# Grouped queries laid 8 apart: moves of rotated halves in runs of 1 KB, score weights read with that stride

## The chip, the cores and the metric

The kernel runs on one core of a Trainium2 chip. Its time is the device time of one execution in microseconds (us). TensorE (PE in the profile) does the matrix products; each product consists of a load of its stationary operand (LDWEIGHTS, on the row PEld) and the stream of the moving operand through the array (MATMUL, on the row PE). VectorE (DVE), ScalarE (ACT) and GpSimd (POOL) do the rest, and SyncE (SP) issues most of the DMAs, one after the other in a queue of its own (SPq).

## The reference

Two layers over x of 16 sequences of 256 tokens and width 256, all in float32. Each layer computes `x + s * silu(f)` from the normalised x. In layer 0, s is a linear recurrence with 32 complex states and f a two-layer feed-forward network. In layer 1, s is causal attention with 16 heads and f a base product plus low-rank experts. What matters here is the attention of layer 1:

```python
q = (x @ Wq).reshape(B, S, N_HEADS, QK_DIM)
q_nope, q_rope = (q[..., :QK_NOPE], q[..., QK_NOPE:])
q = jnp.concatenate([q_nope, apply_rope(q_rope)], axis=-1)
...
scores = jnp.einsum('bqhd,bkhd->bhqk', q, k) * scale
mask = jnp.tril(jnp.ones((S, S), dtype=bool))
attn = jax.nn.softmax(scores, axis=-1)
out = jnp.einsum('bhqk,bkhd->bqhd', attn, v).reshape(B, S, N_HEADS * V_DIM)
```

The keys of all heads come from one latent of 64 numbers per token and one rotated part of 64, so that the kernel folds the head's key matrix into its query: a query is then 64 latent numbers and two rotated halves of 32, which makes 128 numbers, one per partition.

## The kernel before, in words

The 4096 tokens are cut into 8 chunks of 512 (two sequences each). Layer 0 runs first, for about 270 us; then layer 1 goes through the chunks. Each chunk has four **groups** of 4 heads, and each group has two **units**, one for each of the chunk's two sequences: 64 units in all. The program order of every engine is written out by hand: `InOrder` (lines 45 to 65) chains the instructions of an engine in the order in which they are written, and because it records each of them, nearly all of them carry line 53 in the profile. Instructions are therefore told apart by the tiles they write and read.

**Making the queries of a group** (lines 378 to 426). `query_mm` computes four products of 512 columns: t = 0 and 1 are the two rotated halves of the four heads (32 partitions for a head), t = 2 and 3 the latent parts of two heads each. `query_mul` (DVE) multiplies the rotary halves with cosines and sines; `query_rot` (POOL) adds and subtracts them into the tile `qrot`, of 2 x 512 numbers in each of 128 partitions. `query_lat` (ACT) scales the latent parts out of PSUM straight into the tile `qg`, partitions 0 to 63. The rotated halves lie in `qrot` with one head in 32 partitions, and must go to partitions 64 to 127 of `qg`, one head beside the other: `query_move` does that with eight DMAs on SP's queue, one for each half and head.

`qg` is laid out as 16 blocks of 32 queries, and within a block by head: `[P, CH // 32, G, 32]`. The 128 queries of one block and four heads lie next to each other, and a move writes runs of 32 numbers (128 bytes).

**Scores** (`score_pack`, lines 1354 to 1384). In a unit, block a of 32 queries needs the first 32 (a + 1) keys. The product has the 4 x 32 queries of the block as its stationary operand (a load of 128 columns) and the keys as its moving operand (32 to 256 columns). The eight blocks go in three packs, each into one PSUM bank: blocks 7 and 6; 5, 4 and 3; 2, 1 and 0. A float32 product is run as two passes, each with a load of its own, so that the profile has 1024 loads and 1024 matmuls for the 64 x 8 blocks. DVE then masks and takes the maxima, ACT the exponentials, POOL divides (`normalise`), DVE transposes squares of 32 x 32 (`turn`), and two DMAs by way of a DRAM buffer, `send` (lines 1411 to 1418) and `fetch` (line 1423), finish the transposition. `values` multiplies with the latents two units later, and `finish_mm` and `fast_mm` apply the output weights.

**Order** (the loop at lines 1603 to 1694). An even unit runs pack 0, `query_mm(n, 3)`, pack 1, the DMAs of `send` and then of `query_move`, `values` of two earlier units, pack 2. An odd unit runs pack 0, `query_mm(n, 0)`, pack 1, `query_mm(n, 1)`, pack 2, `query_mm(n, 2)`, and POOL does `query_rot` at its end. Smaller pieces (gates, routers, keys, the output product) stand between units. A group's queries are begun three units before its first pack 0. SP's queue holds, per unit, one fetch and four sends, and per group eight moves.

Of the kernel before, what the change touches and what calls it, by code (L numbers as in the profile page):

```python
# [11 lines left out]
F32 = mybir.dt.float32  # L12
I32 = mybir.dt.int32
AF = mybir.ActivationFunctionType
ALU = mybir.AluOpType
# [3 lines left out]
P = 128  # L19
B, S, D = 16, 256, 256  # L20
NTOK = B * S
CH = 512
# [19 lines left out]
def tile_two_layers(ctx: ExitStack, tc: tile.TileContext, d: dict, out: bass.AP):  # L42
# [158 lines left out]
    def bc(ap, n):  # L201

        return ap.unsqueeze(1).to_broadcast([ap.shape[0], n, ap.shape[1]])
# [11 lines left out]
    qr = ctx.enter_context(tc.tile_pool(name="qr1", bufs=1))  # L215
    qp = ctx.enter_context(tc.tile_pool(name="q1", bufs=2))
# [4 lines left out]
    gp = InOrder(nc.gpsimd)  # L221
    place = {}

    def m1(name, shape):
        return place["pool"].tile(shape, F32, tag=place["tag"], name=name)
# [142 lines left out]
    G = 4  # L368
    NG = NH // G
    NQ = S // 32  # L370
    SCALE = 1.0 / math.sqrt(NOPE + ROPE)
# [6 lines left out]
    def query_mm(n, t):  # L378
        q = groups[n]
        ch, g = divmod(n, NG)  # L380
        k = chunks[ch]
        if t == 0:
            q.qg = qp.tile([P, CH // 32, G, 32], F32, tag="qg", name=f"qg_{n}")
            q.rot = qr.tile([P, 2, CH], F32, tag="qrot", name=f"qrot_{n}")
            q.mul, q.ps = [None, None], [None] * 4
        q.ps[t] = ps = m1(f"pq_{n}_{t}", [P, CH])
        for c in range(2):
            if t < 2:
                w = wrope[:, c, g, t, :, :].rearrange("p h f -> p (h f)")
            else:  # L390
                h0 = g * G + 2 * (t - 2)
                w = wlat[:, c, h0 : h0 + 2, :]
            pe.matmul(ps, w, k.xnT[:, c, :], start=(c == 0), stop=(c == 1))

    def query_mul(n, t):
        q = groups[n]
        q.mul[t] = m = qm.tile([P, 2, CH], F32, tag="qmul", name=f"qmul_{n}_{t}")
        for r in range(2):
# [3 lines left out]
                bc(rot_q[:, r, :], 2), ALU.mult,  # L402
            )

    def query_lat(n, t):
        q = groups[n]
        for hh in range(2):
            ac.mul(
                q.qg[0:64, :, 2 * (t - 2) + hh, :],
                q.ps[t][64 * hh : 64 * hh + 64, :].rearrange("p (a q) -> p a q", q=32), SCALE,  # L410
            )

    def query_rot(n):
        q = groups[n]
        m0, m1_ = q.mul
        gp.tensor_tensor(q.rot[:, 0, :], m0[:, 0, :], m1_[:, 1, :], ALU.subtract)
        gp.tensor_tensor(q.rot[:, 1, :], m1_[:, 0, :], m0[:, 1, :], ALU.add)

    def query_move(n):
        q = groups[n]  # L420
        for r in range(2):
            for h in range(G):
                sp.dma_start(
                    q.qg[64 + 32 * r : 96 + 32 * r, :, h, :],
                    q.rot[32 * h : 32 * h + 32, r, :].rearrange("p (a q) -> p a q", q=32),
                )


    with ExitStack() as l0:
# [106 lines left out]
        def tiny(name, n=1):  # L536
            return w0.tile([P, n], F32, tag=name, name=name)
# [44 lines left out]
        f = tiny("f")  # L582
# [24 lines left out]
        for k in range(8):  # L607
            n = 1 << k
# [125 lines left out]
        def recur_out(ch, g, w, ve, ge):  # L734

            swapped(w, g)
            h = a2.tile([P, S], F32, tag="hs", name=f"hs_{ch}")
            ve.tensor_tensor(h, g, ct, ALU.mult)
            ge.tensor_tensor(h, h, w, ALU.subtract)
            return h  # L740
# [476 lines left out]
        o = out1  # L1217
        for ch in range(FIRST, NCH - 1):
            xn, xnT, norm2, o = middle(ch, xn, xnT, norm2, fill, o)
# [5 lines left out]
        t = 2 * ch - 1  # L1225
# [27 lines left out]
        h = recur_out(ch, g, w, v0, g0)  # L1253
        zf = mix(ch, 0, hT, v=v0, a=a0)
        router_chunk(0)
        key_chunk(0)
        outs(ch, h, dx, v0)
        query_mm(0, 0)
        query_mul(0, 0)
        query_mm(0, 1)  # L1260
        query_mul(0, 1)
        finish0(ch, 0, dx, zf, g0)
        query_rot(0)
        query_move(0)
        for jp in range(2):
            finish0(ch - 1, jp, z6.dx, z6.z[jp], v0)
        zf = mix(ch, 1, hT, v=v0, a=a0)
        ve.tensor_scalar(bb_bc, bb_bc, 0.5, None, ALU.mult)
        query_mm(0, 2)
        query_lat(0, 2)  # L1270
        query_mm(0, 3)
        query_lat(0, 3)
        norm_end(1)
        query_mm(1, 0)
        query_mul(1, 0)
        query_mm(1, 1)
        query_mul(1, 1)
        finish0(ch, 1, dx, zf, g0)
        query_rot(1)
        query_mm(1, 2)  # L1280
        query_lat(1, 2)


# [70 lines left out]
    def score_pack(u, pi):  # L1354
        k, b, pack = chunks[u.ch], u.b, PACK[pi]
        if pi == 0:
            u.nm = sm1.tile([P, NQ], F32, tag="nm", name=f"nm_{u.n}", bufs=3)
            u.sr = sm1.tile([P, NQ], F32, tag="sr", name=f"sr_{u.n}", bufs=3)
        qg = groups[u.i // 2].qg
        sc = ps_sc.tile([P, CH], F32, tag="sc", name=f"sc_{u.n}_{pi}")  # L1360
        for a, o in pack:
            pe.matmul(
                sc[:, o : o + 32 * (a + 1)], qg[:, b * NQ + a, :, :].rearrange("p h q -> p (h q)"),
                k.kT[:, b * S : b * S + 32 * (a + 1)], start=True, stop=True,
            )
        ends = [o + 32 * (a + 1) for a, o in pack]
        step = ends[1] - ends[0]
        n = len(pack)
        assert ends == [ends[0] + step * z for z in range(n)]
        if ends[0] - 32 + step * n <= CH:  # L1370
            diag = sc[:, ends[0] - 32 : ends[0] - 32 + step * n].rearrange("p (n s) -> p n s", n=n)[:, :, 0:32]
        else:
            diag = sc[:, ends[0] - step : ends[-1]].rearrange("p (n s) -> p n s", n=n)[:, :, step - 32 : step]
        ve.tensor_tensor(diag, diag, bc(kmask, n), ALU.add)
        for a, o in pack:
            ve.tensor_reduce(
                u.nm[:, a : a + 1], sc[:, o : o + 32 * (a + 1)], AX.X, ALU.max, negate=True
            )
        for a, o in pack:
            w = 32 * (a + 1)  # L1380
            ac.activation(
                u.pr[:, OFF[a] : OFF[a] + w], sc[:, o : o + w], AF.Exp,
                bias=u.nm[:, a : a + 1], accum_out=u.sr[:, a : a + 1],
            )
# [218 lines left out]
    for i in range(LAST):  # L1603
        ch, r = divmod(i, PER)
# [3 lines left out]
        n = (i + 3) // 2 if odd else (i + 2) // 2  # L1608
        n = n if n < len(groups) else None
# [4 lines left out]
        if 2 <= i:  # L1614
            fetch(units[i - 2])
        score_pack(u, 0)
        if w:
            normalise(w, (2,))
# [30 lines left out]
        if i == 5:  # L1649
            values(units[1])  # L1650
        score_pack(u, 1)

        if odd and n is not None:
            query_mm(n, 1)
            query_mul(n, 0)
        if i == 2:
            query_move(n)
# [6 lines left out]
        if not odd:  # L1664
            if n is not None and i != 2:
                query_move(n)
            if i >= 4:
                values(units[i - 4])
            if i > 4:
                values(units[i - 3])  # L1670
        score_pack(u, 2)
        normalise(u, (0, 1))

        if odd and n is not None:
            query_mm(n, 2)
            query_mul(n, 1)
            query_rot(n)
            query_lat(n, 2)
# [111 lines left out]
```

## Time and profile before

| | |
|---|---|
| time, median of 3 runs | 921.83 us (920.75 to 923.23) |
| span of the profiled execution | 919.9 us |
| PE busy | 905.2 us, 98% of the span |
| PEld busy | 695.4 us, 76% |
| DVE, ACT, POOL busy | 72%, 51%, 62% |
| idle time of PE within the span | 14.7 us |
| DMA packets | 196412, of which 142112 are under 512 bytes |

The profile is of one execution, and its span is the time from its first to its last instruction. The page gives no other time of that execution; the median of the runs shown is 1.9 us above the span. PE's clock is granted in full from the first slices on (9 of 9 in tenths, 0.98 to 1.00 in every stretch after 60 us). The DMA engines are nearly idle between 60 and 270 us, and about 73% busy from 340 to 880 us. A busy share of PE is not a share of its peak: matmuls overlap, so the time that one of them adds is read from the distance between the starts of two, not from its own duration.

### The profile page before, as it was taken

The numbers are of one execution on the slowest core, as the hardware profiler recorded it, in microseconds if no ns is written. First come the engines' busy times: TensorE is split into PE (matmuls) and PEld (weight loads), VectorE is DVE, ScalarE is ACT, GpSimd is POOL, SyncE is SP. The second block draws the span as 40 slices with busy tenths as digits, with TensorE's granted clock in tenths as the row PEclk, the third lists the DMA queues.
The fourth block names the chain that finished last, engine by engine and source line by source line (L and its number), as shares of the span: only waits on it lengthen the run. The fifth ranks groups of instructions, "written<-read, shape, count | busy, mean of one in ns | idle before, by whom it ended". The sixth has DMA issues, their size and how long they took to land.

```text
span 919.9 us, 17382 instructions
## 1 busy us (share of the span) xinstructions
PE 905.2 (98%) x5426; PEld 695.4 (76%) x5426; DVE 666.4 (72%) x2018; ACT 465.8 (51%) x1529; POOL 570.6 (62%) x885
## 2 busy tenths in 40 slices
PE   8999999999999899999999999999999999999998
PEld 7768898987767567777777777777777777777776
DVE  6876687664688779668967866896786689677562
ACT  3335555654336545645644564564466456446541
POOL 1228697777355537686586767648676764866541
PEclk9999999999999999999999999999999999999999
DMA  9730000000025777777776777777677777767771
GB/s 280 232 115 1 1 2 1 1 2 1 1 32 106 201 203 184 203 186 186 178 210 160 208 194 192 189 178 207 159 209 206 181 190 178 205 160 211 206 224 42
DMA packets 196412, 134.00 MB, mean 146 GB/s; under 512 B 142112, under 2 KB 186976, under 8 KB 196320
## 3 DMA queue, kind: packets, MB, share of 16 engines
q1 hardware_dynamic: 194192, 128.68, 53.3%
q0 software_dynamic: 1152, 3.67, 1.2%
q8 instruction: 44, 0.72, 0.3%
q10 hardware_dynamic: 976, 0.53, 0.2%
q14 instruction: 48, 0.39, 0.1%
HBM read 63.11 MB, written 52.95 MB: 126 GB/s over the span
## 4 chain that ended last, share of the span: by engine, by line
PE 90%; DVE 3%; DMA 2%; SPq 2%; POOL 1%; issue 1%; ACT 0%; POOLq 0%; DVEq 0%; ACTq 0%
PE pq L53 22%; PE sc L53 14%; PE po L53 10%; PE av L53 9%; PE r L53 7%; PE f L53 7%; PE ph L53 5%; PE pf L53 5%; PE pg L53 4%; PE pm L53 2%; SPq L53 2%; PE pkv L53 1%; PE tp L53 1%; DMA qg<-qrot 1%; PE py L53 1%; PE pb L53 1%
## 5 line engine op out<-in xcount | busy, mean ns | idle before, releaser
L53 ACT ACTIVATE pr<-sc,nm 128x256 f32<-128x256 f32 (+7 forms) x512 | 189.7, 381 | 240.3 <-DVE sr L53 152.2
L53 POOL TENSOR_SCALAR pr<-pr,sr 128x256 f32<-128x256 f32 (+7 forms) x512 | 192.1, 394 | 190.0 <-DVE sr L53 184.1
L53 PEld LDWEIGHTS sc<-kT,qg 128*128 128x128 f32 x1024 | 157.6, 191 | 62.3 <-issue 40.3
L53 PE MATMUL sc<-kT,qg 128*128 128x256 f32 (+7 forms) x1024 | 176.1, 306 | 5.7 <-DMA qg<-qrot 4.4
L53 DVE TENSOR_REDUCE nm<-sc 128x1 f32<-128x256 f32 (+7 forms) x512 | 127.5, 301 | 6.6
L53 DVE STREAM_TRANSPOSE turned<-pr 128x512 f32<-128x512 f32 x186 | 123.2, 687 | 9.6 <-POOL pr L53 8.7
L53 PE MATMUL pq<-xnT,wlat 128*128 128x512 f32 x256 | 124.1, 608 | 0.0
L53 PE MATMUL pq<-xnT,wrope 128*128 128x512 f32 x256 | 120.2, 593 | 0.0
L53 ACT ACTIVATION_READ_ACCUMULATOR pr<-sc,nm 128x1 f32 x512 | 104.3, 204 | 0.0
L53 DVE TENSOR_TENSOR sc<-sc,kmask 128x96 f32<-128x96 f32 (+1 forms) x192 | 45.5, 237 | 64.9 <-PE sc L53 63.9
L53 PE MATMUL av<-pT,row 128*64 128x256 f32 (+1 forms) x1024 | 90.9, 329 | 0.5 <-DMA pT<-far 0.5
L53 POOL TENSOR_TENSOR qrot<-qmul,qmul 128x512 f32<-128x512 f32 x64 | 83.0, 1317 | 8.0 <-POOL pr L53 2.9
L53 PEld LDWEIGHTS av<-pT,row 128*64 128x64 f32 x1024 | 64.1, 137 | 24.3 <-issue 1.6
L53 DVE TENSOR_TENSOR qmul<-pq,rot_q 128x512 f32<-128x512 f32 x128 | 80.7, 672 | 0.1
L53 ACT ACTIVATE qg<-pq 64x512 f32<-64x512 f32 x128 | 75.4, 589 | 5.4 <-PE pq L53 4.7
L53 PEld LDWEIGHTS pq<-xnT,wlat 128*128 128x128 f32 x256 | 46.0, 192 | 32.0 <-issue 32.0
L53 PEld LDWEIGHTS pq<-xnT,wrope 128*128 128x128 f32 x256 | 45.7, 191 | 32.4 <-issue 32.1
L53 PEld LDWEIGHTS po<-wout,attT 128*128 128x128 f32 x416 | 58.4, 191 | 9.5 <-issue 4.9
L53 PE MATMUL po<-wout,attT 128*128 128x128 f32 (+1 forms) x416 | 64.5, 308 | 0.0
L53 POOL TENSOR_TENSOR rs<-ve,mhalf 128x4 f32<-128x4 f32 (+1 forms) x17 | 16.8, 986 | 51.3 <-DVE ve L53 37.0
L53 PE MATMUL ph<-xnT,p1T 128*128 128x256 f32 (+1 forms) x128 | 44.3, 503 | 0.8 <-DVE xnT L53 0.8
L53 POOL TENSOR_TENSOR attT<-attT,attT 128x512 f32<-128x512 f32 x36 | 45.0, 1270 | 0.0
(226 smaller groups left out, 1505.0 us busy)
## 6 DMA issues: line engine op xcount, KB each, us to landing
far<-turned SPq DMA_DIRECT2D x248, 192.0 KB, 4.3
pT<-far SPq DMA_DIRECT2D x62, 768.0 KB, 5.0
qg<-qrot SPq DMA_DIRECT2D x256, 64.0 KB, 2.3
x<-in_x_dram SPq DMA_DIRECT2D x7, 512.0 KB, 9.3
out_dram<-x POOLq DMA_DIRECT2D x12, 256.0 KB, 4.9
wqn_wo<-in_wq_nopeT_dram SPq DMA_DIRECT2D x4, 512.0 KB, 4.9
wqn_wo<-in_Wo_dram SPq DMA_DIRECT2D x4, 512.0 KB, 6.1
p2T<-in_proj2T_dram SPq DMA_DIRECT2D x2, 512.0 KB, 7.2
```

The source lines that it names most:

```text
L53: r = getattr(self.engine, name)(*args, **kw)
```

## The change

`qg` becomes `[P, 2, G, S]`: for each sequence and head a run of 256 queries in each partition, with query 32 a + q at place 8 q + a. The 32 queries of block a are thus 8 numbers (32 bytes) apart. `qrot` takes the same order, so that a move copies runs of 256 numbers (1 KB) on both sides. The 128 stationary columns of a score product (four heads of 32 queries) are then read with a step of 8 numbers; the step goes on evenly from one head to the next, since a head is 256 = 32 x 8 numbers long. ACT (`query_lat`) and POOL (`query_rot`) read as before, block after block, and write with a step of 8 numbers. Number, kind and order of the instructions of all engines stay as they are.

```diff
         if t == 0:
-            q.qg = qp.tile([P, CH // 32, G, 32], F32, tag="qg", name=f"qg_{n}")
-            q.rot = qr.tile([P, 2, CH], F32, tag="qrot", name=f"qrot_{n}")
+            q.qg = qp.tile([P, 2, G, S], F32, tag="qg", name=f"qg_{n}")
+            q.rot = qr.tile([P, 2, 2, S], F32, tag="qrot", name=f"qrot_{n}")
...
+    def strided(ap):
+
+        return ap.rearrange("p b (q a) -> p b a q", a=NQ)
+
+    def blocks(ap):
+
+        return ap.rearrange("p (b a q) -> p b a q", b=2, q=32)
+
     def query_lat(n, t):
         q = groups[n]
         for hh in range(2):
             ac.mul(
-                q.qg[0:64, :, 2 * (t - 2) + hh, :],
-                q.ps[t][64 * hh : 64 * hh + 64, :].rearrange("p (a q) -> p a q", q=32), SCALE,
+                strided(q.qg[0:64, :, 2 * (t - 2) + hh, :]),
+                blocks(q.ps[t][64 * hh : 64 * hh + 64, :]), SCALE,
             )
 
     def query_rot(n):
         q = groups[n]
         m0, m1_ = q.mul
-        gp.tensor_tensor(q.rot[:, 0, :], m0[:, 0, :], m1_[:, 1, :], ALU.subtract)
-        gp.tensor_tensor(q.rot[:, 1, :], m1_[:, 0, :], m0[:, 1, :], ALU.add)
+        r0, r1 = (strided(q.rot[:, r]) for r in range(2))
+        gp.tensor_tensor(r0, blocks(m0[:, 0, :]), blocks(m1_[:, 1, :]), ALU.subtract)
+        gp.tensor_tensor(r1, blocks(m1_[:, 0, :]), blocks(m0[:, 1, :]), ALU.add)
 
     def query_move(n):
...
                 sp.dma_start(
-                    q.qg[64 + 32 * r : 96 + 32 * r, :, h, :],
-                    q.rot[32 * h : 32 * h + 32, r, :].rearrange("p (a q) -> p a q", q=32),
+                    q.qg[64 + 32 * r : 96 + 32 * r, :, h, :], q.rot[32 * h : 32 * h + 32, r]
                 )
...
             pe.matmul(
-                sc[:, o : o + 32 * (a + 1)], qg[:, b * NQ + a, :, :].rearrange("p h q -> p (h q)"),
+                sc[:, o : o + 32 * (a + 1)],
+                qg[:, b].rearrange("p h (q a) -> p a (h q)", a=NQ)[:, a],
                 k.kT[:, b * S : b * S + 32 * (a + 1)], start=True, stop=True,
             )
```

## The prediction

> **What bounds the kernel now.** I read the page's busy times first, then TensorE's waits, then the chain of work through two units.
>
> ```profile
> PE 905.2 (98%) x5426; PEld 695.4 (76%) x5426; DVE 666.4 (72%) x2018; ACT 465.8 (51%) x1529; POOL 570.6 (62%) x885
> ```
>
> TensorE (PE) is busy all but 14.7 us of the 919.9 us span, and no other engine comes near. Its waits:
>
> ```profile
> PE sc L53 <- DMA qg<-qrot: 4.4, 2, 3.5
> ...
> PE sc L53 <- ACT pr L53: 1.3, 1, 1.3
> ...
> PE av L53 <- DMA pT<-far: 0.5, 1, 0.5
> ```
>
> The moves that the change speeds up make TensorE wait twice, for 4.4 us in all, both times before 400 us. Everything DMA costs TensorE is 4.9 us. So the change can gain half a per cent at most, and what matters is whether it makes TensorE's own work longer. The chain (start, us, what) shows how that work is spaced in an odd unit:
>
> ```profile
> 350.53 0.81 PE sc L53 x4
> 351.34 1.72 PE pq L53 x4
> 353.06 0.82 PE sc L53 x6
> 353.88 1.72 PE pq L53 x4
> 355.60 0.59 PE sc L53 x6
> ```
>
> The four pq matmuls stream 512 columns each and take 1.72 us: 0.84 ns per column. By that, pack 0 (256, 256, 224, 224 columns) needs 0.81 us and pack 1 (192, 160, 128, each twice) also 0.81; the chain has 0.81 and 0.82. Pack 2 (96, 64, 32, each twice) would need 0.32 but takes 0.59: it waits for its weight loads.
>
> ```profile
> 355.44 0.64 PEld L53 LDWEIGHTS sc<-kT,qg 128*128 128x128 f32 x5 [0.24 <-issue]
> 355.99 0.30 PEld L53 LDWEIGHTS pq<-xnT,wlat 128*128 128x128 f32 x2
> ```
>
> Five loads start within 0.55 us, 110 ns apart. A load runs beside the matmul ahead of it, so a step from one matmul to the next lasts as long as the longer of that matmul's stream and the next load.
>
> **Part 1, the strided weights.** 1024 loads of 128 columns now read words 32 bytes apart. Contiguous loads cost, by form:
>
> ```profile
> L53 PEld LDWEIGHTS sc<-kT,qg 128*128 128x128 f32 x1024 | 157.6, 191 | 62.3 <-issue 40.3 <-ACT pr L53 8.5 <-ACT qg L53 4.3
> L53 PEld LDWEIGHTS av<-pT,row 128*64 128x64 f32 x1024 | 64.1, 137 | 24.3 <-issue 1.6 <-PE av L53 0.7
> ```
>
> 64 more columns take 191 - 137 = 54 ns: 0.84 ns per column, 108 for the load. No row of this trace has an operand of the array with a step, so the price needs bounds.
> - Below: 0.84 ns per column as now. Nothing is gained, since the columns are as many.
> - Above: one further fetch per column, as slow as the slowest word in any row. GpSimd's two-input operations need (1267 - 726) / 256 = 2.11 ns per element for two words (rows below), 1.06 per word. 0.84 + 1.06 = 1.90 ns, 243 ns a load.
> - I take a second fetch at the array's own pace, 2 x 0.84 = 1.69 ns, 216 ns a load. With the step no two columns of a load lie side by side, and the nearest row with two fetches per element is GpSimd's 2.11.
>
> [...]
>
> With loads of 216 ns, by the step rule, at 0.84 ns per column:
> - Pack 0: streams 215, 215, 188, 188; the following loads 216, 216, 216 and a contiguous 108. Steps 216 x 3 + 188 = 836 ns, 30 more than 806.
> - Pack 1: five steps of 216 and a last of 108 make 1188, 382 more than 806.
> - Pack 2: five of 216 and one of 108 make 1188; before, six of 108 were 648. 540 more.
> - The first load of a pack. Ahead of pack 1 always, and of pack 2 in odd units, stands a pq stream of 430 ns: hidden. Ahead of pack 2 in even units stand the `values` matmuls (2.75 us for 32): 108 more, 54 on average. Ahead of pack 0 stand 128-column matmuls (108 ns streams) in 6 of 8 units: 81 on average.
>
> Sum 1087 ns per unit; 64 units: **+69.6 us**, all on TensorE's path. At the ends: nothing, and, at 243 ns, 111 + 517 + 675 + 108 + 68 = 1479 ns, +94.7 us.
>
> **Part 2, the moves.** Each of 256 issues becomes cheaper on SP's queue. I compare the moves with the four loads of `rot_q`, which have the shape of the new moves (32 partitions with runs of 1 KB):
>
> ```profile
> L53 SPq DMA_DIRECT2D qg<-qrot x256: 585/628/2102, 261.6 to 878.7; - x128
> ...
> L165 SPq DMA_DIRECT2D rot_q<-in_rope_q_dram x4: 414/420/582, 30.2 to 31.7; - x4
> ```
>
> About 0.21 us less each, 1.5 us over the seven issues between a move's first and last. Packets fall from 512 per move to 64, 114688 fewer of 196412. The waits of 3.5 and 0.9 us become 2.0 and 0: a gain of 2.4. Landing takes 2.3 us now and 1.9 for `rot_q`; with less traffic for all others the ends are -2.4 and all DMA waits, -4.9. With an unchanged TensorE I take the middle, **-3.6**. If part 1 slows TensorE by a microsecond per unit, everything that feeds it is earlier by that, and both waits on the moves go: **-4.4**.
>
> [...]
>
> **Part 3, strided writes of ACT and POOL.** Rows now:
>
> ```profile
> L53 ACT ACTIVATE qg<-pq 64x512 f32<-64x512 f32 x128 | 75.4, 589 | 5.4 <-PE pq L53 4.7
> ```
>
> ```profile
> L53 POOL TENSOR_TENSOR qrot<-qmul,qmul 128x512 f32<-128x512 f32 x64 | 83.0, 1317 | 8.0 <-POOL pr L53 2.9 <-DVE qmul L53 2.8 <-DMA qg<-qrot 2.2
> ...
> L53 POOL TENSOR_SCALAR pr<-pr,sr 128x256 f32<-128x256 f32 x64 | 30.6, 478 | 133.8 <-DVE sr L53 128.0 <-DMA qg<-qrot 4.1 <-DMA pT<-far 0.5
> ...
> L53 POOL TENSOR_TENSOR c<-c,g 128x256 f32<-128x256 f32 x12 | 8.7, 725 | 0.0
> ```
>
> Nothing below today's time is possible, since elements and passes stay. Above, one more 0.84 ns for each of 512 elements is +0.43 us: 128 x 0.43 = 55 us on ACT, 64 x 0.43 = 28 us on POOL. I take the upper end and cost it at nothing: on ACT the exponentials queued behind wait 240.3 us in all for DVE, on POOL the divisions 190.0 us, and a group's queries are begun three units before use. Per group ACT would work 1.7 us more in about 20 us. If the cover is gone, up to 55 us come to the end; maxima and PSUM banks for scores would be late next.
>
> **The sum.** On the profiled execution: 919.9 + 69.6 - 4.4 = 985.1. The median of the runs is 1.9 above the span: **987.0 us**.
>
> **Rivals.**
> 1. *Strided loads cost nothing* (the other side). The moves are then all that changes: 921.8 - 3.6 = 918.2, between 916.9 and 919.4. For it: a load takes one word per column at 0.84 ns, contiguous or not, and no row shows that neighbours help. Against it: every row of the trace reads neighbours. Per nanosecond of longer load a unit loses 5 (pack 2), 1 (the end of pack 1) and 1.25 (first loads); 3.6 us over 64 units are 56 ns, so it decides at a load of 116 ns, 0.90 ns per column.
> 2. *Half a fetch more*, midway between none and one: 162 ns. Pack 0 stays, pack 1 +112, pack 2 +270, first loads +67: 449 ns per unit, 28.7 us, 946 us. For it: part of a fetch may lie under the one before. [...]
> 3. *The cover of part 3 is gone*: up to 55 us with free loads, 973. Against it: ACT and POOL idle for hundreds of microseconds.
> 4. *The moves gain nothing* because TensorE hardly waits for them and their landing is a fixed cost; with free loads that is 921.8.
>
> **Numbers.** Forecast 0.40, rival 1 0.35, rival 2 0.14, rival 3 and loads beyond 243 ns 0.08, rival 4 0.03. Range: from rival 1's lower end, 916, to the bound of 243 ns, 921.8 + 94.7 - 4.4 = 1012. Alone, the forecast's case is 975 to 1012. A difference under 0.3%, 2.8 us, cannot be told from no change. Rival 1 straddles that at 919.1: 0.26 faster, 0.09 same. With rival 4: faster 0.26, same 0.12, slower 0.62.
>
> **What would show it.** The mean of the score loads: 191 ns now, about 299 if right, 191 in rival 1. The chain's packs: 0.84, 1.19 and about 1.13 us against 0.81, 0.82, 0.59; only packs 1 and 2 may grow, and matmul rows of pq stay at 1.72 per four. Move issues near 420 ns; packets near 82000; TensorE's waits for `qg` gone. `qg` near 1.02 us on ACT at most. I am wrong if the score loads keep 110 ns of spacing, or if TensorE shows new idle time behind ACT or DVE.

## The result, and the profile after

The changed kernel takes 1000.71 us (median of 4 runs, 1000.18 to 1001.77) against 922.53 us (median of 4 runs beside it): 1.0848 times the time before, with a 95% interval of 1.0833 to 1.0864. It is 78 us slower. The forecast was 987.0 us, in a range of 916 to 1012.

The page's busy times and TensorE's waits in the changed kernel:

```profile
PE 988.9 (99%) x5426; PEld 797.3 (80%) x5426; DVE 664.7 (67%) x2018; ACT 535.2 (54%) x1529; POOL 573.0 (57%) x885
```

```profile
PE tp L53 <- DVE xn L53: 1.9, 1, 1.9
PE warm L53 <- POOL ident masks.py:199: 1.5, 1, 1.5
PE pmT L53 <- ACT qg L53: 1.4, 1, 1.4
PE ph L53 <- DVE xnT L53: 0.8, 1, 0.8
```

The span grew from 919.9 to 998.4 us, by 78.5. TensorE's busy time grew by 83.7 us and its idle time fell by 5.2. No wait for a move is left, and no new wait behind DVE, ACT or POOL has come; the one that grew is that of `pmT` for ACT's part of a query, from 0.5 to 1.4 us. TensorE did not get its work later, the work itself got longer. The chain shows which work (start, us, what; an odd unit again):

```profile
357.30 0.93 PE sc L53 x4
358.23 1.72 PE pq L53 x4
359.94 1.30 PE sc L53 x6
361.24 1.72 PE pq L53 x4
362.96 1.22 PE sc L53 x6
```

The pq products are where they were, at 1.72 us for four. The three packs of scores went from 0.81, 0.82 and 0.59 us to 0.93, 1.30 and 1.22. Pack 2, with the shortest streams, was the shortest and now takes nearly as long as pack 1: both have six loads, and the streams no longer count. The weight loads say so themselves (timelines of the load row and of the matmul row, and the groups by form):

```profile
362.37 1.69 PEld L53 LDWEIGHTS sc<-kT,qg 128*128 128x128 f32 x6 [0.24 <-issue]
363.97 0.32 PEld L53 LDWEIGHTS pq<-xnT,wlat 128*128 128x128 f32 x2
```

```profile
362.80 1.38 PE L53 MATMUL sc<-kT,qg 128*128 128x96 f32 x6
```

```profile
L53 PEld LDWEIGHTS sc<-kT,qg 128*128 128x128 f32 x1024 | 265.2, 330 | 39.2 <-issue 21.3 <-ACT pr L53 3.7 <-DVE eq L53 1.7
L53 PEld LDWEIGHTS av<-pT,row 128*64 128x64 f32 x1024 | 64.0, 137 | 23.7 <-issue 1.6
```

The first of the six loads lies beside a stream of 512 columns; the chain starts the pack at 362.96, and the timeline has its first matmul at 362.80. The other five start between there and 363.97, where the next load follows: 234 ns each, where it was 110. The mean load went from 191 to 330 ns. The loads of `av`, which are contiguous, stayed at 137.

The issues of the moves (min, median and max of one in ns), the page's line of DMA packets, and its groups of the two engines that now write with a step:

```profile
L53 SPq DMA_DIRECT2D qg<-qrot x256: 585/595/1835, 261.1 to 951.9; - x128
```

```profile
DMA packets 81724, 134.00 MB, mean 134 GB/s; under 512 B 11040, under 2 KB 72288, under 8 KB 81632
```

```profile
L53 ACT ACTIVATE qg<-pq 64x512 f32<-64x512 f32 x128 | 141.4, 1105 | 2.3 <-PE pq L53 1.5
...
L53 POOL TENSOR_TENSOR qrot<-qmul,qmul 128x512 f32<-128x512 f32 x64 | 81.7, 1300 | 2.8 <-DVE qmul L53 2.8
```

The packets fell by 114688 as counted, yet an issue takes 595 ns in the median where it took 628, not 420. ACT's writes nearly doubled (589 to 1105 ns); POOL's hardly changed (1317 to 1300).

### The profile page after: what moved, and what is told of

Same layout as the page of the kernel before. It is cut to its first block, busy times and chain, and to the rows that moved or that the text cites. A ratio compares the mean times of both kernels' runs of the same rounds, so it can differ in the third digit from the quotient of the medians.

```text
span 998.4 us, 17382 instructions
## 1 busy us (share of the span) xinstructions
PE 988.9 (99%) x5426; PEld 797.3 (80%) x5426; DVE 664.7 (67%) x2018; ACT 535.2 (54%) x1529; POOL 573.0 (57%) x885
## 3 DMA queue, kind: packets, MB, share of 16 engines
q1 hardware_dynamic: 79504, 128.68, 44.6%
## 4 chain that ended last, share of the span: by engine, by line
PE 98%; DVE 1%; DMA 0%; ACT 0%; POOL 0%; issue 0%; SPq 0%; POOLq 0%
PE sc L53 24%; PE pq L53 22%; PE po L53 10%; PE av L53 9%; PE r L53 6%; PE f L53 6%; PE ph L53 4%; PE pg L53 4%; PE pf L53 4%; PE pm L53 2%; PE pkv L53 2%; PE tp L53 1%; PE py L53 1%; PE pb L53 1%; PE psq L53 1%; PE pso L53 0%
## 5 line engine op out<-in xcount | busy, mean ns | idle before, releaser
L53 POOL TENSOR_SCALAR pr<-pr,sr 128x256 f32<-128x256 f32 (+7 forms) x512 | 195.5, 401 | 264.1 <-DVE sr L53 262.6
L53 PEld LDWEIGHTS sc<-kT,qg 128*128 128x128 f32 x1024 | 265.2, 330 | 39.2 <-issue 21.3
L53 PE MATMUL sc<-kT,qg 128*128 128x256 f32 (+7 forms) x1024 | 262.8, 391 | 0.0
L53 ACT ACTIVATE qg<-pq 64x512 f32<-64x512 f32 x128 | 141.4, 1105 | 2.3 <-PE pq L53 1.5
L53 DVE TENSOR_TENSOR sc<-sc,kmask 128x96 f32<-128x96 f32 (+1 forms) x192 | 47.5, 248 | 139.7 <-PE sc L53 138.1
L53 ACT ACTIVATION_READ_ACCUMULATOR pr<-sc,nm 128x1 f32 x512 | 102.1, 199 | 0.0
```

The lines of the kernel that those rows point to most:

```text
L53: r = getattr(self.engine, name)(*args, **kw)
```

## The experiments

The theory, called S: a load whose columns do not lie side by side takes longer for each column, and that alone makes the difference. Its refinement, L, an assumption of the author's until the steps were run (e4 to e6): what counts is how many columns fall into one piece of 16 bytes (a line, in the expectations). The first rivals put the longer loads down to something else that the change brought (W), or the loss to ACT's longer writes (A).

### One part alone: the loads (e1), and all but the loads (e2)

e1 is the kernel before, with

```diff
-                sc[:, o : o + 32 * (a + 1)], qg[:, b * NQ + a, :, :].rearrange("p h q -> p (h q)"),
+                sc[:, o : o + 32 * (a + 1)], qg[:, b * NQ : (b + 1) * NQ].rearrange("p a h q -> p (a h q)").rearrange("p (c z) -> p z c", z=8)[:, a],
```

> The kernel before with one change: a score load reads its 128 columns with a step of 8 numbers (32 bytes). It thereby takes columns of eight blocks at once, so that the scores are those of other queries; their number and the work are the same. Moves, ScalarE and GpSimd as before. Theory S (the step of the read alone makes the load longer): mean of the score loads 330 ns as after, packs 0, 1 and 2 near 1.0, 1.3 and 1.2 us, time 998 to 1006 us. Rival W (the loads are longer because of who writes the tile now: ScalarE's writes with a step and moves of 1 KB that collide with the loads): loads 191 ns, time 920 to 925 us.

e2 is the changed kernel, with

```diff
-                qg[:, b].rearrange("p h (q a) -> p a (h q)", a=NQ)[:, a],
+                qg[:, b].rearrange("p h s -> p (h s)")[:, P * a : P * (a + 1)],
```

> The changed kernel with one thing undone: a score load reads 128 adjacent columns. It thereby takes other queries than those of its block; their number and the work are the same. The moves of 1 KB and the strided writes of ScalarE and GpSimd stay. Theory S: loads 191 ns, time 916 to 922 us, although ScalarE's writes into qg stay at 1.1 us. Rival W: loads 330 ns, time about 1000 us. Rival A (ScalarE's longer writes delay the exponentials): loads 191 ns, TensorE has new idle time, time 930 to 975 us.

Measured: e1 1000.49 us, 1.0847 [1.0824, 1.0871]; e2 919.85 us, 0.9967 [0.9955, 0.9980]. The loads by form, of e1 and then of e2:

```profile
L53 PEld LDWEIGHTS sc<-kT,qg 128*128 128x128 f32 x1024 | 265.2, 330 | 39.2 <-issue 21.1 <-ACT pr L53 3.8 <-DVE eq L53 1.7
```

```profile
L53 PEld LDWEIGHTS sc<-kT,qg 128*128 128x128 f32 x1024 | 157.7, 191 | 60.4 <-issue 40.2 <-ACT pr L53 12.0 <-DVE eq L53 1.7
```

The step of the read alone gives the whole ratio of the change, 1.0847 beside 1.0848, and everything else in the change gives a small gain. W has fallen: in e1 the tile is written as before and the loads take 330 ns; in e2 it is written as after and they take 191. e1 and the changed kernel also show that once TensorE is slow, the moves are worth nothing that can be seen: their times lie 0.2 us apart, with runs of 128 bytes and of 1 KB, and e1 has no wait for a move either.

A has fallen as well: 919.85 us is below the 930 that it asks for at least. In e2 ACT's writes take as long as in the changed kernel, 1102 ns in the median, and TensorE's waits are few:

```profile
PE sc L53 <- ACT pr L53: 2.9, 2, 2.7
...
PE pmT L53 <- ACT qg L53: 1.5, 1, 1.5
...
PE sc L53 <- DMA qg<-qrot: 1.0, 1, 1.0
```

A write takes 593 ns in the median before, so that the 128 of them keep ACT 65 us longer in e2, and TensorE's waits behind ACT grow by no more than 2.6 us (2.9 and 1.5 us here, 1.3 and 0.5 before, the last in this row of the kernel before):

```profile
PE pmT L53 <- ACT qg L53: 0.5, 1, 0.5
```

### The moves alone (e3)

```diff
-            q.qg = qp.tile([P, CH // 32, G, 32], F32, tag="qg", name=f"qg_{n}")
+            q.qg = qp.tile([P, 2, G, S], F32, tag="qg", name=f"qg_{n}")
...
-                q.ps[t][64 * hh : 64 * hh + 64, :].rearrange("p (a q) -> p a q", q=32), SCALE,
+                q.ps[t][64 * hh : 64 * hh + 64, :].rearrange("p (b s) -> p b s", b=2), SCALE,
...
-                    q.rot[32 * h : 32 * h + 32, r, :].rearrange("p (a q) -> p a q", q=32),
+                    q.rot[32 * h : 32 * h + 32, r, :].rearrange("p (b s) -> p b s", b=2),
...
-                sc[:, o : o + 32 * (a + 1)], qg[:, b * NQ + a, :, :].rearrange("p h q -> p (h q)"),
+                sc[:, o : o + 32 * (a + 1)], qg[:, b].rearrange("p h s -> p (h s)")[:, P * a : P * (a + 1)],
```

> The kernel before with the moves alone changed: qg and qrot in the plain order of the tokens, runs of 1 KB in the moves, contiguous writes of ScalarE and GpSimd, and score loads of 128 adjacent columns (of other queries than those of the block; the work is the same). What the moves are worth without their price: 916.9 to 919.4 us by the prediction's first rival, TensorE's 4.4 us of waits for the moves gone or below 2. Rival M (the moves gain nothing): 921 to 923 us, the waits as before.

Measured: 918.05 us, 0.9942 [0.9924, 0.9961]. This is what the change could have brought: 5.6 us, within its interval 3.6 to 7.0. TensorE's waits:

```profile
PE sc L53 <- DMA qg<-qrot: 2.3, 1, 2.3
```

Half of the 4.4 us of waits for moves went, where below 2 us had been expected to stay. The issues got only 33 ns cheaper and landing went from 2.3 to 2.0 us, so that moves still come late once. The 5.6 us are a difference of medians; the two profiled executions differ by 2.7 us (spans of 919.9 and 917.2), and what else the medians contain was not traced. The difference between e2 and e3 (what the strided writes of ACT and POOL cost) lies within the intervals of the two, which overlap, and is not shown.

### How the price depends on the step (e4, e5, e6)

Each is e1 with another step. In place of e1's new line stands, for 2, 3 and 4:

```diff
+                sc[:, o : o + 32 * (a + 1)], qg[:, b * NQ : (b + 1) * NQ].rearrange("p a h q -> p (a h q)").rearrange("p (w c z) -> p w z c", z=2, c=P)[:, a % 4, a % 2],
+                sc[:, o : o + 32 * (a + 1)], qg[:, b * NQ : (b + 1) * NQ].rearrange("p a h q -> p (a h q)")[:, 0:3 * P].rearrange("p (c z) -> p z c", z=3)[:, a % 3],
+                sc[:, o : o + 32 * (a + 1)], qg[:, b * NQ : (b + 1) * NQ].rearrange("p a h q -> p (a h q)").rearrange("p (w c z) -> p w z c", z=4, c=P)[:, a % 2, a % 4],
```

> As e1 with a step of 2 numbers (8 bytes; scores of other queries, the same work). [...] Rival G (the price grows with the step): loads 205 to 240 ns, time 930 to 955 us. Rival N (any step other than 1 costs the same): loads 330 ns, about 1003 us.

> As e1 with a step of 3 numbers (12 bytes; scores of other queries, the same work). [...] Rival T (a step under 16 bytes is free, as step 2 nearly was): loads 197 ns, 922 to 926 us.

> As e1 with a step of 4 numbers (16 bytes; scores of other queries, the same work). Theory L: every column opens a line, as with step 8: loads 330 ns, time 998 to 1003 us. Rival G (the price grows with the distance): loads 220 to 280 ns, 930 to 970 us.

The rows of the loads, of e4, e5 and e6 in turn:

```profile
L53 PEld LDWEIGHTS sc<-kT,qg 128*128 128x128 f32 x1024 | 162.7, 197 | 60.0 <-issue 39.6 <-ACT pr L53 8.8 <-ACT qg L53 4.2
```

```profile
L53 PEld LDWEIGHTS sc<-kT,qg 128*128 128x128 f32 x1024 | 206.4, 258 | 48.5 <-issue 34.9 <-ACT pr L53 10.2 <-DVE eq L53 1.7
```

```profile
L53 PEld LDWEIGHTS sc<-kT,qg 128*128 128x128 f32 x1024 | 260.0, 324 | 39.7 <-issue 20.6 <-ACT pr L53 4.1 <-DVE eq L53 1.7
```

| step, numbers (bytes) | mean load, ns | more than contiguous | time, us | ratio |
|---|---|---|---|---|
| 1 (4), before | 191 | | 922.13 | 1 |
| 2 (8), e4 | 197 | 6 | 923.72 | 1.0016 [1.0001, 1.0031] |
| 3 (12), e5 | 258 | 67 | 951.10 | 1.0314 [1.0297, 1.0331] |
| 4 (16), e6 | 324 | 133 | 995.52 | 1.0794 [1.0777, 1.0811] |
| 8 (32), e1 | 330 | 139 | 1000.49 | 1.0847 [1.0824, 1.0871] |

(The median of before is 922.13 us beside e5, e6, e7 and e8; beside e1 to e4 it was 923.62, and their ratios go by that.) The price is no step function of "strided or not" (rival N), nor does it go on growing with the distance (rival G): from 16 to 32 bytes it goes from 133 to 139 ns. Step 3 decides between L and the threshold of rival T. Of four columns 12 bytes apart, two fall into one piece of 16 bytes and two are alone in theirs; a load then costs 67 ns more, half of the 133 to 139 that it costs when all are alone. The estimate by L ahead of e5 was 261 ns, the 191 of a contiguous load and half of e1's 139, and 945 to 965 us; 258 ns and 951.10 us were measured. Two figures of L were missed by a little: with a step of 2 the load is 6 ns longer than before, not equal, and with a step of 4 it takes 324 ns and 995.52 us, not 330 and 998 to 1003.

The four steps fit pieces of 16 bytes; they do not exclude another law, and how a load comes by its longer time no run shows. A price that rises evenly between 8 and 16 bytes and then stays would give the same rows, since 12 bytes is half way. Columns in adjacent pairs with wide gaps between the pairs would tell the two apart, and no run has them.

### The moving operand (e8)

```diff
-                k.kT[:, b * S : b * S + 32 * (a + 1)], start=True, stop=True,
+                k.xnT.rearrange("p c (n z) -> p z (c n)", z=4)[:, b, 0 : 32 * (a + 1)], start=True, stop=True,
```

> The kernel before with contiguous score loads, but with the moving operand read with a step of 4 numbers (16 bytes), out of another tile of the chunk (the normalised tokens in place of the keys; widths and count of the matmuls are the same). If the price belongs to reading a new line per column, whichever operand it is: the streams go from 0.84 to about 1.83 ns per column, 1152 columns twice per unit and 64 units, about 125 us more, 1035 to 1055 us; loads 191 ns. Rival (it belongs to the weight load alone): 920 to 925 us.

Measured: 1032.56 us, 1.1195 [1.1177, 1.1212], just under the range expected; the mean load is 200 ns where 191 was expected. The matmuls by form (busy us, mean ns), of e8 and then of the kernel before:

```profile
L53 PE MATMUL sc<-xnT,qg 128*128 128x256 f32 x128 | 68.2, 622 | 0.0
...
L53 PE MATMUL sc<-xnT,qg 128*128 128x128 f32 x128 | 40.6, 406 | 0.0
...
L53 PE MATMUL sc<-xnT,qg 128*128 128x32 f32 x128 | 21.1, 254 | 0.0
```

```profile
L53 PE MATMUL sc<-kT,qg 128*128 128x256 f32 x128 | 38.7, 384 | 5.7 <-DMA qg<-qrot 4.4 <-ACT pr L53 1.3
...
L53 PE MATMUL sc<-kT,qg 128*128 128x128 f32 x128 | 24.6, 274 | 0.0
...
L53 PE MATMUL sc<-kT,qg 128*128 128x32 f32 x128 | 23.1, 262 | 0.0
```

Here it is the wide streams that grow, and the 32-column ones, which wait for contiguous loads, do not. From 128 to 256 columns the busy time of one matmul rises by (68.2 - 40.6) / 128 = 216 ns, 1.69 ns per column, twice the 0.84 of contiguous streams. The chain, which goes by distances, has a little more:

```profile
410.47 1.69 PE sc L53 x4
412.16 1.72 PE pq L53 x4
413.88 1.70 PE sc L53 x6
...
417.30 0.72 PE sc L53 x6
```

Packs 0 and 1 stream 960 columns each, in 1.69 and 1.70 us: 1.76 and 1.77 ns per column. The other tile is not the reason, since the pq matmuls stream that same tile side by side and keep their 1.72 us. So the price is not one of the load alone; it was paid on either operand: 234 / 128 = 1.83 ns per column of the load with a step of 32 bytes, 1.76 per column of the stream with one of 16. The 125 us expected are 0.84 ns more for each of the 147456 columns, not the 0.99 that 1.83 would make. The range was too high all the same: pack 2, whose short streams lie beside loads, grew by only 0.13 us (0.59 to 0.72), and TensorE's waits fell by 7.0 us (10.9 to 3.9 in all).

### A layout between the two (e7)

With the price known, a layout offers itself that keeps two columns in each piece of 16 bytes: only two blocks are interleaved, and the moves have runs of 256 bytes. This is the changed kernel with

```diff
-            q.qg = qp.tile([P, 2, G, S], F32, tag="qg", name=f"qg_{n}")
-            q.rot = qr.tile([P, 2, 2, S], F32, tag="qrot", name=f"qrot_{n}")
+            q.qg = qp.tile([P, 2, 4, G, 64], F32, tag="qg", name=f"qg_{n}")
+            q.rot = qr.tile([P, 2, 2, 4, 64], F32, tag="qrot", name=f"qrot_{n}")
...
-        return ap.rearrange("p b (q a) -> p b a q", a=NQ)
+        return ap.rearrange("p b c (q z) -> p (b c) z q", z=2)
...
-                qg[:, b].rearrange("p h (q a) -> p a (h q)", a=NQ)[:, a],
+                qg[:, b, a // 2].rearrange("p h (q z) -> p z (h q)", z=2)[:, a % 2],
```

(The lines left out give `blocks`, `query_lat` and `query_move` the same new shape.)

> The reference's computation in a layout between the two kernels: only two blocks are interleaved, so that the 32 queries of a block are 2 apart, score loads step by 8 bytes, moves have runs of 256 bytes, and ScalarE and GpSimd write with a step of 8 bytes. Theory S with L: loads 197 ns, which costs 1 to 2 us, and the moves give back part of the 5.6 us of e3: 918 to 922 us, ratio 0.996 to 1.000. ScalarE's writes: 0.59 us if their price too is that of a line per element, 1.1 us if any step costs. Rival: time at or above before (1.000 to 1.005), because runs of 256 bytes bring nothing.

Measured: 920.93 us (12 runs) against 922.13 (17 runs), 0.9985 [0.9975, 0.9996]. It beats both kernels, the one before by 1.2 us (0.4 to 2.3 by the interval), which is a small part of what e3 gives. Loads take 196 ns, ACT's writes 637 ns in the median where contiguous ones take 593, packets fall to 130876 as counted (256 fewer in each of 256 moves). TensorE's longest wait in e7:

```profile
PE sc L53 <- ACT qg L53: 2.7, 1, 2.7
```

The waits for moves are gone from this profile, and one wait of 2.7 us for ACT's part of the queries stands in their place. The plain order of e3 with a block's own queries would need loads of four runs of 32 columns, 256 numbers apart; that was not tried.

## Why the prediction was right, and where it was off

**The bound.** Right: TensorE's own work sets the time, before and after (busy for 98% and 99% of the span), and only what lengthened it counted.

**Part 1, the strided weights.** The cause was right, shown by e1 (the loads alone give the ratio) and e2 (without them it is gone). The step rule held: pq streams unchanged, pack 0 longer by 0.12 us, packs 1 and 2 by 0.48 and 0.63 in the odd units shown. What was mis-sized is the load: 216 ns taken, 234 measured in the trace, within the bounds of 108 and 243 but nearer the upper one. With 234 the prediction's sum per unit is 84 ns for pack 0, 472 and 630 for packs 1 and 2, and 95 and 63 for the first loads of packs 0 and 2: 1344 ns, 86 us over 64 units. (The trace of before has a matmul of 136 columns or fewer ahead of pack 0 in 41 of 64 units, not in 6 of 8; that takes 1 us off.) The score matmuls' busy time did grow from 176.1 to 262.8 us, by 86.7. The choice of twice the pace was an argument without a row behind it, and it came near: the loads pay 234 / 128 = 1.83 ns per column and e8's streams 1.76, where 1.69 was taken. That there is a second fetch, as the argument had it, no run shows; what the runs show in place of its 216 ns is a load that takes 234. Nor does the upper bound have anything to do with the array: it comes from GpSimd's rows, by the median of 1267 ns where the row shown has a mean of 1317 (which would give 256 ns a load), so that the measured value lay inside by some luck. In the sum at 243 ns the first loads of pack 0 should be 101 ns by the prediction's own rule, not 108; that changes 94.7 us by 0.4.

By step, a load took 6 ns more with 8 bytes (e4), 67 with 12 (e5), 133 with 16 (e6) and 139 with 32 (e1). That fits a count of the columns in a piece of 16 bytes, though the even rise named above would fit as well. Loads of columns side by side went by the number of columns (64 more of them cost 54 ns, from 137 to 191); with as many columns 32 bytes apart a load took 139 ns more.

**Part 2, the moves.** The gain of 3.6 us with an unchanged TensorE was 5.6 in e3, with an interval of 3.6 to 7.0. The working behind it was wrong in one step: an issue does not cost 420 ns because its runs are 1 KB long. It is 595 ns in the median with 64 packets and 628 with 512, and its minimum is 585 in both. The four loads of `rot_q` do not have the shape of the new moves, though the prediction says so: each writes 32 runs of 1 KB (line 165), a move 64, one for each of 32 partitions and two sequences. Two other loads of `rot_q` write 64 such runs, and in the kernel before their issues took 491 ns (line 162) and 597 ns (line 163), nearer to what the moves took. All six loads come from DRAM; whether that matters, too, was not tried. Landing came to 2.0 us against the 1.9 taken. That in the slow case both waits on the moves go was right, and so was the reason, a slower TensorE: in e1, with the moves of before, they are gone as well. TensorE's idle time fell by 5.2 us where 4.4 was taken. The 86.7 us less 5.2 would make 81.5; the span grew by 78.5. The remaining 3 us are busy time that other matmuls have less in the profile (83.7 instead of 86.7), which is not explained further.

**Part 3, strided writes.** Costing them at nothing was right as far as the runs can tell: the changed kernel and e1 lie 0.2 us apart, e2 and e3 1.8. Their sizes were not: ACT pays 516 ns for 512 elements, 1.01 ns per element, above the bound of 0.84; POOL pays next to nothing (means of 1317 and 1300 ns, medians of 1267 and 1288).

**The rivals.** Rival 1 is what e2 and e3 show when the loads are contiguous, 919.85 and 918.05 us; it fell to the measured 234 ns, far beyond its point of decision at 116. Rival 2, 946 us, is near what a step of 3 numbers took (e5, 951 us), not one of 8. Rival 3 fell too: its cover held, since with ACT's longer writes TensorE's waits behind ACT grew by 2.6 us at most (e2). Rival 4 fell with e3, whose gain is clear of zero; nor was landing a fixed cost, since it went from 2.3 to 2.0 us.

## What to carry to other kernels

Before a matmul's operand is given a step, stationary or moving, look at the step in bytes: with float32 a step of 2 (8 bytes) was nearly free here (6 ns a load, e4), and a step of 4 (16 bytes) took a load from 191 to 324 ns (e6) and a stream from 0.84 to 1.76 ns per column (e8). Where short matmuls stood in a row, the longer load was paid in full (pack 2 of an odd unit went from 0.59 to 1.22 us, with five loads 124 ns further apart); beside a stream of 512 columns it cost nothing (pq kept its 1.72 us). And read first how much TensorE waits for a transfer at all: here the profile showed 4.9 us and e3 gained 5.6, against 1024 loads that each could become longer.

## What the runs showed that had not been expected

- ACT's writes with a step of 32 bytes take 1105 ns for 512 elements where contiguous ones take 589, and with a step of 8 bytes 637 in the median (e7); POOL's writes take 1288 ns in the median with a step of 32 bytes and 1278 with one of 8 (e7) where they took 1267.
- The issue of a move between partitions of SBUF took SP 585 ns at least, with 512 packets (128 bytes) and with 64 (1 KB) alike. With an eighth of the packets in each move, the DMA queue's share went from 53.3% to 44.6% of a longer span, and landing from 2.3 to 2.0 us.
